# Mixture-of-experts layer of a graph network: the first aggregation's sums accumulated while the count matrix is still being filled, and the loads at the start reordered

## The chip, the cores and the metric

The kernel runs on one core of a Trainium2 chip. The metric is the device time of one execution in microseconds (us). TensorE (PE) multiplies matrices, VectorE (DVE) and ScalarE (ACT) work on elements, GpSimd (POOL) issues the indirect DMAs here, and SyncE (SP) and ACT issue the plain ones. PEld is the loading of weights into TensorE.

## The reference

Four graph layers follow one another on N = 6250 nodes with D = 128 features and 106250 edges, sorted by destination (50000 pairs in both directions and one loop per node). `src`, `dst` and `edge_type` are given.

```python
h = relu(layernorm(x))
x = x + L0(h)    # relu(segsum((h[src] + rel_emb[type]) @ Wn, dst) / sqrt(deg) + h @ W_loop)
h = relu(layernorm(x))
x = x + L1(h)    # mixture of experts, below
h = relu(layernorm(x))
x = x + L2(h)    # edge weights sigmoid(relu((h[dst]-h[src]) @ W1 + b1) @ w2 + b2)
h = relu(layernorm(x))
x = x + L3(h)    # three rounds of normalised mean aggregation

def L1(x):                       # 3 layers, H = 256, 4 weak and 4 strong experts
    h = x @ W_in + b_in
    for l in range(3):
        agg = segsum(h[src], dst) / deg
        logits = concat(h, agg) @ router_W[l] + router_b[l]
        # the two best experts of each node, softmax of their logits as gates
        moe = sum over the two of gate * expert(agg)
        h = h + sigmoid(h @ conf_W[l] + conf_b[l]) * moe
    return h @ W_out + b_out
```

## The kernel before, in words

**The count matrix.** All sums over edges are done as dense matrix products. The nodes are padded to 49 tiles of 128 (`NT`), and the destinations are cut into 13 blocks of 512 (`BW`, `NBLK`; the last has one tile). `adj` in device memory holds, for each block of destinations, a matrix of bytes: how many edges go from each source to each destination. An aggregation of a block loads groups of four source tiles (`AG1`, 256 KB, tile `ra_in`), turns bytes into numbers (`ra_r`, of type F32R), and multiplies each source tile's features with it. The features stand as two halves, a rounded one and the rest (`h2r`, `r2`), so that each tile costs two matmuls: 98 per block and 128 features.

**The first stage** (L302 to L576) makes the matrix and the first graph layer together. The matrix is cleared by SP (`clear`, L331, four DMAs of 784 KB per block from the tile `rzero`), two blocks ahead of the small loads, the rest after them. VectorE computes for each edge its place and its count (`places`, L429; 52 groups of 16 x 128 edges), with keys that ACT's queue loads (L409). POOL writes them with 832 indirect DMAs of 128 edges each (`scatter`, L462), from the last group to the first. A load of block b waits for the scatters that reach it. The loop over the blocks (L499) goes from the last to the first: the count of edge types per destination (`ct`, L512 to L525, some 79 matmuls behind one-hot tiles `oht` and `ohd` that VectorE makes), the degrees (L535 to L551), the aggregation (L553, `aggregate` at L262, whose casts are all on ACT at L276 there), the types' share (L283), a turning of h by TensorE (`transposed`, L286), the two products by weights (L567, L568), and x plus the result, whose normalised rows become `h` (L576). The output of the block's x goes to `x_d[0]`.

Before the loop, x is loaded as one tile `h` (L307, L308) by SP ahead of the first clears, normalised in place in seven steps of 7 tiles, and split into the halves `h2r` (L491 to L494).

**The mixture** (L582 to L948). For each of three layers, `first_step` (L601) goes over the blocks: `load` (L758) fetches `ra_in` on SP, VectorE and ACT share the casts (L801, L803), TensorE sums (L807; one part of 128 features in layer 0, which aggregates before the product by `W_in`, and two in the layers after). `inputs` (L608) makes h turned, `aggregated` (L636) scales the sums and in layer 0 multiplies them by `W_in` (L653), and `rest` (L658), a generator, does the routing: logits (`plt`, L665; turned into `plg`, L672), the two best experts (L684 to L711), the number of rows ahead of each (`pk`, L728, L729), and POOL's writes of the rows into the experts' lists (L743). The generator of block b - 1 is advanced among the groups of block b. In layer 0 the halves `r2` are made by `rows` (L767) from `h`; in the later layers the rows are loaded from `hf_d`, and `inputs` loads the block again as `rold` (L788) and transposes it (L632). `second_step` (L821) runs the experts over their lists.

**Order.** The program is written as a stream of tile operations; a scheduler at build time puts them into one fixed sequence per engine, by priority (in the order of the program, `tc.high_priority()` ahead) and by its own model of durations, and sets the waits. Each engine then runs its sequence in order. So an instruction that waits holds all that stands behind it on its engine or its queue. A pool (`tc.tile_pool`) gives memory back when it closes, and a tile that takes this memory waits for its last users.

The edge stage (L1033 on) uses `tloc` (L1059), made from `dloc`, the place of each edge's destination in its window, that the first stage kept.

## Time and profile before

| | |
|---|---|
| median of 3 runs | 6091.3 us (6075.11 to 6093.58) |
| profiled execution | 6081.65 us, span of its instructions 6079.9 us |
| PE busy | 4834.3 us (80%), 24167 instructions |
| DVE, ACT, POOL busy | 3079.4 us (51%), 2516.0 us (41%), 2525.5 us (42%) |
| mean granted TensorE clock | 0.901 |
| first scatter, last scatter (L465) starts | 54.9, 1155.4 us |
| router of layer 0: first aggregation matmul, last matmul of `first_step` (L924) | 1231.8, 1675.7 us |

The profile's groups give a line of the kernel, an engine, the operation with the tiles it writes and reads, the count, then the busy time and the mean of one in ns, and after the second bar the idle time of the engine just before these instructions with what ended it. Busy matmuls overlap, so the distance between starts says more than a mean duration. The slices of the page cut the span into 40 equal parts; each digit is a share in tenths. The clock is the share of TensorE's full rate that was granted.

### The profile page before, as it was taken

The numbers are of one execution on the slowest core, as the hardware profiler recorded it, in microseconds if no ns is written. First come the engines' busy times: TensorE is split into PE (matmuls) and PEld (weight loads), VectorE is DVE, ScalarE is ACT, GpSimd is POOL, SyncE is SP. The second block draws the span as 40 slices with busy tenths as digits, with TensorE's granted clock in tenths as the row PEclk, the third lists the DMA queues.
The fourth block names the chain that finished last, engine by engine and source line by source line (L and its number), as shares of the span: only waits on it lengthen the run. The fifth ranks groups of instructions, "written<-read, shape, count | busy, mean of one in ns | idle before, by whom it ended". The sixth has DMA issues, their size and how long they took to land. (4 is left out here: it accounts for less than half of the span.)

```text
span 6079.9 us, 76269 instructions
## 1 busy us (share of the span) xinstructions
PE 4834.3 (80%) x24167; PEld 3639.6 (60%) x24191; DVE 3079.4 (51%) x7850; ACT 2516.0 (41%) x5902; POOL 2525.5 (42%) x2376
## 2 busy tenths in 40 slices
PE   0186345599978899997879998986577878789999
PEld 0143223366656677775657776665556666678887
DVE  8975345554511333331133332116788888875555
ACT  2153233344322222222222222224678878855444
POOL 5777777422254211114521112361777777600000
PEclk9987677799989999998989998998678878899999
DMA  8234334455464533335653334467566666534454
GB/s 308 84 63 133 81 111 117 122 147 157 142 146 74 128 94 100 101 90 131 120 139 99 98 97 136 81 119 208 151 177 200 194 184 205 172 89 126 129 147 138
DMA packets 605630, 811.31 MB, mean 133 GB/s; under 512 B 116102, under 2 KB 402616, under 8 KB 605084
## 3 DMA queue, kind: packets, MB, share of 16 engines
q1 hardware_dynamic: 372740, 549.03, 30.5%
q0 software_dynamic: 132896, 194.37, 14.7%
q10 hardware_dynamic: 99448, 61.48, 3.8%
q8 instruction: 239, 3.92, 0.3%
q14 instruction: 307, 2.51, 0.2%
HBM read 594.70 MB, written 209.89 MB: 132 GB/s over the span
## 5 line engine op out<-in xcount | busy, mean ns | idle before, releaser
L807 PE MATMUL ragg<-ra_r,r 128*128 128x512 f32 (+1 forms) x6370 | 1471.5, 388 | 11.4 <-ACT r L777 10.5
L807 PEld LDWEIGHTS ragg<-ra_r,r 128*128 128x128 f32 x6370 | 1153.6, 190 | 270.9 <-issue 30.3
L1128 POOL DMA_INDIRECT rss<-rtab_s,rsrc_c x832 | 809.0, 972 | 376.5 <-DMA rx_d<-rv 111.5
L465 POOL DMA_INDIRECT adj<-rcnt,ixs x832 | 816.5, 981 | 285.6 <-issue 247.2
L743 POOL DMA_INDIRECT list_d<-rx,rpli x294 | 313.7, 1067 | 1439.0 <-issue 1184.5
L276 ACT CAST ra_r<-ra_in 128x1024 fp32r<-128x1024 uint8 (+3 forms) x494 | 543.9, 1113 | 776.5 <-DMA ra_in<-adj 422.2
L801 DVE CAST ra_r<-ra_in 128x1536 fp32r<-128x1536 uint8 (+4 forms) x507 | 388.0, 768 | 843.5 <-PE ragg L807 701.0
L803 ACT CAST ra_r<-ra_in 128x1024 fp32r<-128x1024 uint8 (+3 forms) x468 | 371.7, 797 | 1025.9 <-PE ragg L807 658.3
L882 POOL DMA_INDIRECT hf_d<-ry,rto x352 | 548.0, 1557 | 552.2 <-DVE ry L868 343.4
L279 PE MATMUL ragg<-ra_r,h 128*128 128x512 f32 (+1 forms) x1274 | 388.2, 447 | 324.9 <-ACT ra_r L276 324.9
L279 PEld LDWEIGHTS ragg<-ra_r,h 128*128 128x128 f32 x1274 | 241.6, 213 | 347.8 <-ACT ra_r L276 329.8
L1161 PE MATMUL acc<-mv,oh 128*128 128x258 f32 x1648 | 347.3, 354 | 112.4 <-DVE mv L1155 110.9
L274 DVE CAST ra_r<-ra_in 128x1024 fp32r<-128x1024 uint8 (+4 forms) x364 | 268.6, 744 | 249.9 <-PE ragg L279 237.1
L1161 PEld LDWEIGHTS acc<-mv,oh 128*128 128x128 f32 x1648 | 290.3, 238 | 152.9 <-DVE mv L1155 144.3
L1086 PE MATMUL rpart<-ra_r,cur 128*128 128x512 f32 (+1 forms) x1144 | 326.5, 413 | 51.7 <-ACT ra_r L1083 41.6
L1141 PE MATMUL pz<-gw,ohT 128*128 128x128 bf16 x2496 | 248.8, 259 | 125.8 <-DVE ohT L1133 69.4
L279 PE MATMUL ragg<-ra_r,cur 128*128 128x512 f32 (+1 forms) x1404 | 327.8, 393 | 6.2 <-DVE ra_r L274 6.2
L523 PE MATMUL ct<-ohd,oht 128*128 128x128 bf16 (+7 forms) x1024 | 204.9, 222 | 159.1 <-DVE ohd L521 149.5
L866 PE MATMUL rp<-st,rsh 128*128 128x256 f32 x1344 | 315.1, 383 | 18.3 <-DVE ry L868 18.3
L835 DVE COPY at<-rtr 128x512 f32<-128x512 f32 (+1 forms) x112 | 77.0, 687 | 489.8 <-PE rtr L834 489.8
L856 PE MATMUL rp<-at,st 128*128 128x512 f32 x672 | 302.1, 603 | 2.7 <-DVE roff L846 1.4
L1148 ACT ACTIVATE rz<-rz 128x128 f32<-128x128 f32 x832 | 245.9, 297 | 129.9 <-DVE rz L1144 129.3
(320 smaller groups left out, 7939.3 us busy)
## 6 DMA issues: line engine op xcount, KB each, us to landing
ra_in<-adj SPq DMA_DIRECT2D x1092, 256.0 KB
row<-list_d SPq DMA_DIRECT2D x111, 516.0 KB
list_d<-rzero SPq DMA_DIRECT2D x65, 774.0 KB
adj<-rzero SPq DMA_DIRECT2D x52, 784.0 KB
rd_b<-dst SPq DMA_DIRECT2D x208, 128.0 KB
gw<-rtab_d SPq DMA_DIRECT2D x208, 96.0 KB
adj<-rcnt,ixs POOLq DMA_INDIRECT x832
rss<-rtab_s,rsrc_c POOLq DMA_INDIRECT x832
```

Source lines behind the costliest of these rows:

```text
L276: nc.scalar.copy(ar[:, m:c, :w], a[:, m:c, :w])
L279: nc.tensor.matmul(ps[:, :w], rows2[:, s, g + k, :], ar[:, k, :w], start=(g + k == t0 and s == 0), stop=(not extra and g + k == NT - 1 and ...
L465: d = nc.gpsimd.indirect_dma_start(out=adj[0:(hi + 1) * ABS], out_offset=bass.IndirectOffsetOnAxis(ap=ixs[:, s, j:j + 1], axis=0), in_=cnt ...
L743: d = nc.gpsimd.indirect_dma_start(out=list_d[:], out_offset=bass.IndirectOffsetOnAxis(ap=pli[:, 2 * t + k:2 * t + k + 1], axis=0), in_=xs ...
L801: nc.vector.tensor_copy(ar[:, :m, :w], a[:, :m, :w])
L803: nc.scalar.copy(ar[:, m:c, :w], a[:, m:c, :w])
L807: nc.tensor.matmul(ps[:, h_, :w], r2[:, s, g + k, h_ * P:(h_ + 1) * P], ar[:, k, :w], start=(n == 0 and k == 0 and s == 0), stop=(n == len ...
L866: nc.tensor.matmul(p2_, sh[f][:, t * P:(t + 1) * P], st2[:, f, :], start=(f == 0), stop=False)
L882: d = nc.gpsimd.indirect_dma_start(out=hf_d[:], out_offset=bass.IndirectOffsetOnAxis(ap=to[:, t:t + 1], axis=0), in_=y[:, t, :], in_offset ...
L1086: nc.tensor.matmul(ps[:, :w], cur2[:, s, g + k, :], ar[:, k, :w], start=(g + k == t0 and s == 0), stop=(g + k == t1 - 1 and s == 1))
L1128: nc.gpsimd.indirect_dma_start(out=ss[:, k, 1:], out_offset=None, in_=tab_s[:], in_offset=bass.IndirectOffsetOnAxis(ap=src_c[:, g * WG + k ...
L1161: nc.tensor.matmul(acc[t], oh[:, k, n * P:(n + 1) * P], mv[:, k].rearrange("p s f -> p (s f)"), start=(g == ends[t][0] and k == 0), stop=( ...
```

## The change

* The normalised rows of the first stage's result are kept as two halves `h12` from the start (in place of `h` and, in the mixture's layer 0, `r2`), and a new tile `part1` holds sums of the mixture's first aggregation.
* In the loop of the first stage, `aggregate` is replaced by `sums0` and `more`. `sums0(b)` does the block's own 49 source tiles, and for the sources of blocks that are already done (above b, and not 0 or 1) it uses the same loaded and cast counts for a second sum with `h12`. `more(j, b + 2)` adds to each destination block j from b + 2 up the sources of block b + 2. After the loop, sources 2 to 12 of all destinations are summed. Casts take two tiles at a time (`counts`).
* The mixture's layer 0 sums only the sources of blocks 1 and 0 (`groups = [AG1, 0]`) and adds `part1` in `aggregated`.
* Turning h uses two matmuls with the identity on the two halves (`transposed2`) in place of a transpose, in the first stage and in layer 0; in layers 1 and 2 block 0 is turned from `r2` in this way, and its load `rold` falls away.
* The first clears: block 12, then three of the seven chunks of x (`x_rows`, 7 tiles each), then block 11. The other chunks of x are issued on ACT's queue as buffers come free.
* The identity and the tile of zeros get priority. `iota_f` is made later in a pool of its own, the biases of each mixture layer are built in a pool of their own, `dloc` is no longer kept (the edge stage loads `dst_cols` again), some buffers of the first stage go from two to one.

```diff
     ident = const.tile([P, P], F32, name="rident")
-    make_identity(nc, ident)
...
-    nc.vector.tensor_copy(ident_b, ident)
+    with tc.high_priority():
+        make_identity(nc, ident)
+        nc.vector.tensor_copy(ident_b, ident)
...
     nc.gpsimd.iota(iota8, pattern=[[1, 8]], base=0, channel_multiplier=0,
-                   allow_small_or_imprecise_dtypes=True)
-    iota_f = const.tile([P, P], F32, name="iota_f")
-    nc.gpsimd.iota(iota_f, pattern=[[1, P]], base=0, channel_multiplier=0,
...
     inv_r = const.tile([P, NT], F32, name="rinv_r")
-    dloc = const.tile([P, NCH], F32, name="dloc")
+    ident_r = const.tile([P, P], F32R, name="ident_r")
+    nc.vector.tensor_copy(ident_r, ident)
...
+    def transposed2(dst, rows2, b, psum):
+        nt = blk_tiles(b)
+        p = psum.tile([P, 4, P], F32, tag="mm", name="rtr")
+        for k in range(nt):
+            for s in range(2):
+                nc.tensor.matmul(p[:, k, :], rows2[:, s, 4 * b + k, :], ident_r, start=(s == 0), stop=(s == 1))
+        nc.scalar.copy(dst[:, :nt * P], p[:, :nt, :].rearrange("p t d -> p (t d)"))
...
-    h = hp.tile([P, NT, D], F32, name="rh0")
+    h12 = hp.tile([P, 2, NT, D], F32R, name="h12")
+    part1 = hp.tile([P, NBLK, BW], F32, name="part1")
...
-        nc.vector.memset(h[:, NT - 1, :], 0.0)
-        nc.sync.dma_start(h[:, :NT - 1, :], rows_of(i["x"], 0, NT - 1))
-        nc.sync.dma_start(h[:N - (NT - 1) * P, NT - 1, :], i["x"][(NT - 1) * P:N, :])
...
-        p2 = pool("rprep2", 2)
+        early = ExitStack()
+        p2 = early.enter_context(tc.tile_pool(name="rprep2", reuse_waits="tile", bufs=2))
+        h2r = pp.tile([P, 2, NT, D], F32R, name="h02")
+        XC = 7
+        def x_rows(g, eng):
+            xt = p2.tile([P, XC, D], F32, name="rxt", bufs=3)
+            full = min(XC, NT - 1 - g)
+            eng.dma_start(xt[:, :full, :], rows_of(i["x"], g, full))
+            if full < XC:
+                nc.vector.memset(xt[:, full], 0.0)
+                eng.dma_start(xt[:N - (NT - 1) * P, full, :], i["x"][(NT - 1) * P:N, :])
+            return xt
...
-        for b in (NBLK - 1, NBLK - 2):
-            clear(b)
+        clear(NBLK - 1)
+        xts = [x_rows(g, nc.sync) for g in range(0, 3 * XC, XC)]
+        clear(NBLK - 2)
...
-        h2r = pp.tile([P, 2, NT, D], F32R, name="h02")
...
-        for g in range(0, NT, 7):
-            norm_relu(h[:, g:g + 7], h[:, g:g + 7], 7, p2)
-            nc.scalar.copy(h2r[:, 0, g:g + 7], h[:, g:g + 7])
-            nc.vector.tensor_tensor(h2r[:, 1, g:g + 7], h[:, g:g + 7], h2r[:, 0, g:g + 7], ALU.subtract)
+        for n, g in enumerate(range(0, NT, XC)):
+            xt = xts[n]
+            norm_relu(xt, xt, XC, p2)
+            nc.scalar.copy(h2r[:, 0, g:g + XC], xt)
+            nc.vector.tensor_tensor(h2r[:, 1, g:g + XC], xt, h2r[:, 0, g:g + XC], ALU.subtract)
+            if 3 * XC + g < NT:
+                xts.append(x_rows(3 * XC + g, nc.scalar))
+        early.close()
+        lp = pool("rl0", 2)
...
+        def counts(b, c):
+            w = blk_tiles(b) * P
+            m = blk_tiles(c)
+            a = lp.tile([P, AG1, BW], U8, name="ra_in", tag="a_in", bufs=3)
+            nc.sync.dma_start(a[:, :m], adj_v[b][:, 4 * c:4 * c + m, :])
+            for k in range(0, m, 2):
+                n = min(2, m - k)
+                ar = lp.tile([P, 2, BW], F32R, name="ra_r", tag="a_r", bufs=4)
+                nc.scalar.copy(ar[:, :n, :w], a[:, k:k + n, :w])
+                yield 4 * c + k, [ar[:, q, :w] for q in range(n)]
+        def sums0(b, extra):
+            w = blk_tiles(b) * P
+            ps = ps_a.tile([P, BW], F32, name="ragg0")
+            done = list(range(NBLK - 1, max(b, 1), -1))
+            ps1 = ps_u.tile([P, BW], F32, name="rsum1") if done else None
+            blocks = [c for c in range(NBLK) if c not in done] + done
+            for c in blocks:
+                for t, ars in counts(b, c):
+                    for k, ar in enumerate(ars):
+                        for s in range(2):
+                            nc.tensor.matmul(ps[:, :w], h2r[:, s, t + k, :], ar,
+                                             start=(t + k == 0 and s == 0), stop=False)
+                    if c in done:
+                        for k, ar in enumerate(ars):
+                            for s in range(2):
+                                nc.tensor.matmul(ps1[:, :w], h12[:, s, t + k, :], ar,
+                                                 start=(c == done[0] and t + k == 4 * c and s == 0),
+                                                 stop=(c == done[-1] and t + k == 4 * c + blk_tiles(c) - 1 and s == 1))
+            for k, (lhs, rhs) in enumerate(extra):
+                for s in range(3):
+                    nc.tensor.matmul(ps[:, :w], lhs[:, s, :], rhs, start=False, stop=(k == len(extra) - 1 and s == 2))
+            if done:
+                nc.vector.tensor_copy(part1[:, b, :w], ps1[:, :w])
+            return ps
+        def more(b, c):
+            w = blk_tiles(b) * P
+            ps1 = ps_u.tile([P, BW], F32, name="rsum1")
+            for t, ars in counts(b, c):
+                for k, ar in enumerate(ars):
+                    for s in range(2):
+                        nc.tensor.matmul(ps1[:, :w], h12[:, s, t + k, :], ar, start=(t + k == 4 * c and s == 0),
+                                         stop=(t + k == 4 * c + blk_tiles(c) - 1 and s == 1))
+            if b == c == NBLK - 1:
+                nc.vector.tensor_copy(part1[:, b, :w], ps1[:, :w])
+            else:
+                nc.vector.tensor_tensor(part1[:, b, :w], part1[:, b, :w], ps1[:, :w], ALU.add)
...
-            ps, _ = aggregate(b, lp, ps_a, h2r, 0, 3, [(rel3[:, k], ty[:, k, :w]) for k in range(TYT)], True)
+            if b + 2 < NBLK:
+                for j in range(b + 2, NBLK):
+                    more(j, b + 2)
+            ps = sums0(b, [(rel3[:, k], ty[:, k, :w]) for k in range(TYT)])
...
             nc.vector.tensor_copy(ag[:, :w], ps[:, :w])
-            hT = lp.tile([P, BW], F32, name="rhT0")
-            transposed(hT, h, b, ps_m)
+            hT = lp.tile([P, BW], F32, name="rhT0", bufs=1)
+            transposed2(hT, h2r, b, ps_m)
...
             nc.scalar.dma_start(rows_of(x_d[0], 4 * b, nt), xb[:, :nt])
-            norm_relu(h[:, ts], xb, nt, lp)
+            norm_relu(r, xb, nt, lp)
+            split_halves(h12[:, 0, ts], h12[:, 1, ts], r[:, :nt])
...
     tri = wp.tile([P, P], BF16, name="tri")
-    nc.vector.tensor_scalar(tri, iota_f, iota_p, None, op0=ALU.is_gt)
+    with tc.tile_pool(name="rtri", reuse_waits="tile", bufs=1) as tp:
+        iota_f = tp.tile([P, P], F32, name="iota_f")
+        nc.gpsimd.iota(iota_f, pattern=[[1, P]], base=0, channel_multiplier=0,
+                       allow_small_or_imprecise_dtypes=True)
+        nc.vector.tensor_scalar(tri, iota_f, iota_p, None, op0=ALU.is_gt)
...
                 xT = ap.tile([P, BW], F32, name="rxT")
-                transposed(xT, h, b, ps_m)
+                transposed2(xT, h12, b, ps_m)
...
             else:
-                old = olds[b]
...
+                    fs = slice(f * P, (f + 1) * P)
...
-                        nc.tensor.transpose(p[:, t, :], old[:, t, f * P:(f + 1) * P], ident)
+                        if b:
+                            nc.tensor.transpose(p[:, t, :], olds[b][:, t, fs], ident)
+                            continue
+                        for s in range(2):
+                            nc.tensor.matmul(p[:, t, :], r2[:, s, t, fs], ident_r, start=(s == 0), stop=(s == 1))
...
             u = ap.tile([P, BW], F32, name="ru")
-            nc.vector.tensor_tensor(u[:, :w], ps[:, 0, :w], iv[:, :w], ALU.mult)
+            nc.vector.tensor_tensor(u[:, :w], ps[:, 0, :w], part1[:, b, :w], ALU.add)
+            nc.vector.tensor_tensor(u[:, :w], u[:, :w], iv[:, :w], ALU.mult)
...
-        groups = list(range(0, NT, AG1))
-        if not l:
-            groups.reverse()
+        groups = list(range(0, NT, AG1)) if l else [AG1, 0]
...
             ts = slice(4 * k, 4 * k + nt)
-            if not l:
-                nc.scalar.copy(r2[:, 0, ts], h[:, ts])
-                nc.vector.tensor_tensor(r2[:, 1, ts], h[:, ts], r2[:, 0, ts], ALU.subtract)
-                return
...
             w = nt * P
-            if l:
+            if l and b:
...
                 c = min(AG1, NT - g)
-                if b == 0:
+                if l and b == 0:
...
         bias = wp.tile([P, BW], BF16, name="rbias", bufs=2)
-        bias_rows(bias, [
+        with tc.tile_pool(name=f"rbs{l}", reuse_waits="tile", bufs=1) as bs:
+          bias_rows(bias, [
...
-            (4, 1, slice(8, 9), i["L1_gnn_conf_b"][l:l + 1, :])], BW, wp, "bs")
+            (4, 1, slice(8, 9), i["L1_gnn_conf_b"][l:l + 1, :])], BW, bs, "bs")
...
-            r2 = rp.tile([P, 2, NT, H if l else D], F32R, name=f"r2{l}")
+            r2 = rp.tile([P, 2, NT, H], F32R, name=f"r2{l}") if l else h12
...
         nc.vector.tensor_scalar(base, base, float(NP - P), None, op0=ALU.min)
-        nc.vector.tensor_scalar(base, base, P - 1, None, op0=ALU.bitwise_and)
-        nc.vector.tensor_tensor(tloc, dloc.rearrange("p (g k) -> p g k", k=WG), base, ALU.add)
+        nc.vector.tensor_scalar(base, base, 7, 7, op0=ALU.logical_shift_right, op1=ALU.logical_shift_left)
+        dst_c = ep.tile([P, NWG, WG], I32, name="rdst_c2", bufs=1)
+        nc.sync.dma_start(dst_c.rearrange("p g k -> p (g k)"), i["dst_cols"])
+        nc.vector.tensor_tensor(tloc, dst_c, base, ALU.subtract)
...
```

More of the change, by code (lines that the diff above doesn't have):

```diff
@@ L217, in norm_relu @@
         nc.vector.tensor_scalar(nm[:, :nt], s[:, :nt], -1.0 / D, None, op0=ALU.mult)
-        sq = pool.tile([P, D], F32, name="rln_sq")
         v = small.tile([P, 7], F32, name="rln_v")
         for t in range(nt):
+            sq = pool.tile([P, D], F32, name="rln_sq") if dst is src else dst[:, t, :]
             nc.scalar.activation(sq, src[:, t, :], AF.Square, bias=nm[:, t:t + 1], accum_out=v[:, t:t + 1])
@@ L328, in regular_path @@
         zero = pp.tile([P, zn // 4], F32, name="rzero")
-        nc.vector.memset(zero, 0.0)
+        with tc.high_priority():
+            nc.vector.memset(zero, 0.0)
         def clear(b):
@@ L347, in regular_path @@
             nc.sync.dma_start(dst_c.rearrange("p g k -> p (g k)"), i["dst_cols"])
-            typ_c = cp.tile([P, NCH], I32, name="rtyp_c")
+            typ_c = cp.tile([P, NCH], I32, name="rtyp_c", tag="c")
             nc.sync.dma_start(typ_c, i["typ_cols"])
-            base = cp.tile([P, NWG, WG], I32, name="rbase")
+            base = typ_f.bitcast(I32).rearrange("p (g k) -> p g k", k=WG)
             nc.gpsimd.iota(base, pattern=[[241, NWG], [0, WG]], base=0, channel_multiplier=0)
@@ L354, in regular_path @@
             nc.vector.tensor_scalar(base, base, float(NP - P), None, op0=ALU.min)
-            nc.vector.tensor_tensor(dloc.rearrange("p (g k) -> p g k", k=WG), dst_c, base, ALU.subtract)
-            typ_t = cp.tile([P, NCH], I32, name="rtyp_t")
-            nc.vector.tensor_scalar(typ_t, typ_c, P - 1, None, op0=ALU.bitwise_and)
-            as_number(typ_f.bitcast(I32), typ_t)
-            nc.vector.tensor_scalar(typ_c, typ_c, 7, None, op0=ALU.logical_shift_right)
-            nc.vector.tensor_scalar(typ_c, typ_c, 6.0, 127.0, op0=ALU.mult, op1=ALU.add)
-            nc.vector.tensor_scalar(typ_v.bitcast(I32), typ_c, 23, None, op0=ALU.logical_shift_left)
-            dloc_i = cp.tile([P, NCH], I32, name="dloc_i")
-            nc.vector.tensor_copy(dloc_i, dloc)
-            as_number(dloc_f.bitcast(I32), dloc_i)
-            dst_r = cp.tile([P, NCH], I32, name="rdst_r")
+            nc.vector.tensor_tensor(dst_c, dst_c, base, ALU.subtract)
+            as_number(dloc_f.bitcast(I32), dst_c.rearrange("p g k -> p (g k)"))
+            tv = typ_v.bitcast(I32)
+            nc.vector.tensor_scalar(tv, typ_c, 7, None, op0=ALU.logical_shift_right)
+            nc.vector.tensor_scalar(tv, tv, 6.0, 127.0, op0=ALU.mult, op1=ALU.add)
+            nc.vector.tensor_scalar(tv, tv, 23, None, op0=ALU.logical_shift_left)
+            nc.vector.tensor_scalar(typ_c, typ_c, P - 1, None, op0=ALU.bitwise_and)
+            as_number(typ_f.bitcast(I32), typ_c)
+            dst_r = cp.tile([P, NCH], I32, name="rdst_r", tag="c")
             nc.sync.dma_start(dst_r, i["dst_flat"].rearrange("(p c) -> p c", c=NCH))
@@ L385, in regular_path @@
         QG = 4
-        lp = pool("rl0", 2)
         ps_c = pool("ps_c", 2, space=bass.MemoryType.PSUM)
         ps_a = pool("ps_a0", 1, space=bass.MemoryType.PSUM)
+        ps_u = pool("ps_u0", 2, space=bass.MemoryType.PSUM)
         ps_m = pool("ps_m0", 2, space=bass.MemoryType.PSUM)
@@ L525, in regular_path @@
                                      skip_group_check=True)
-            ci = lp.tile([P, BW], I32, name="rci")
+            ci = lp.tile([P, BW], I32, name="rci", bufs=1)
             nc.vector.tensor_copy(ci[:, :w], ct[:, :w])
-            ty = lp.tile([P, TYT, BW], BF16, name="rty")
+            ty = lp.tile([P, TYT, BW], BF16, name="rty", bufs=1)
             for q in range(TYT):
-                tyi = lp.tile([P, BW], I32, name="rtyi")
+                tyi = lp.tile([P, BW], I32, name="rtyi", bufs=1)
                 nc.vector.tensor_scalar(tyi[:, :w], ci[:, :w], 6 * q, 63, op0=ALU.logical_shift_right,
```

## The prediction

> **What bounds the kernel now.** I first read the slices of the page, then the stretches of 100 us that hold the two stages of the change, then the groups, then single instructions around the hand-over. From the page's slices (152 us each):
>
> ```profile
> PE   0186345599978899997879998986577878789999
> ...
> POOL 5777777422254211114521112361777777600000
> PEclk9987677799989999998989998998678878899999
> ```
>
> Slices 2 to 7 are the first stage: POOL is as busy as it ever is, TensorE half idle and at a lower clock. From slice 8 TensorE is full. The stretches say it more sharply (start and end; busy us and instructions of PE, PEld, DVE, ACT, POOL; clock, DMA share, GB/s):
>
> ```profile
> 700.00:800.00 100.00, 39.54 (x187) 24.27 (x187) 37.77 (x113) 26.59 (x28) 75.00 (x78) 0.67 0.34 93
> 1000.00:1100.00 100.00, 43.41 (x240) 27.11 (x240) 39.67 (x121) 26.64 (x31) 74.33 (x77) 0.72 0.37 89
> ...
> 1400.00:1500.00 100.00, 99.84 (x423) 67.98 (x425) 51.79 (x153) 42.24 (x67) 24.89 (x22) 1.00 0.51 149
> ```
>
> In the first stage no other engine is full and POOL issues 77 scatters per 100 us; its busy 75 us are durations, the gaps of 0.30 us between its instructions make up the rest. In the router stage TensorE leaves nothing free at clock 1.00. The groups name the waits:
>
> ```profile
> L465 POOL DMA_INDIRECT adj<-rcnt,ixs x832 | 816.5, 981 | 285.6 <-issue 247.2
> ...
> L276 ACT CAST ra_r<-ra_in 128x1024 fp32r<-128x1024 uint8 (+3 forms) x494 | 543.9, 1113 | 776.5 <-DMA ra_in<-adj 422.2
> ...
> L279 PE MATMUL ragg<-ra_r,h 128*128 128x512 f32 (+1 forms) x1274 | 388.2, 447 | 324.9 <-ACT ra_r L276 324.9
> ```
>
> Scatter: (816.5 + 285.6)/832 = 1.32 us each, 1102 us in all. ACT waits 422 us for loads of the count matrix (they wait for the scatter of their block) and TensorE waits 325 us for ACT. So stage one is set by POOL, and TensorE has room in it. The end of the stage:
>
> ```profile
> 1155.42 0.96 POOL L465 DMA_INDIRECT adj<-rcnt,ixs  x1 [0.30 <-issue]
> 1205.04 0.59 POOL L192 DMA_DIRECT2D bias_f<-in_L_gnn_weak_b  x1 [48.66 <-DVE rtyi L531]
> ```
>
> ```profile
> 1160.26 1.90 ACT L276 CAST ra_r<-ra_in 128x2048 fp32r<-128x2048 uint8 x1 [28.48 <-DMA ra_in<-adj]
> ```
>
> The last scatter is issued at 1155.4, block 0's first cast starts at 1160.3, and the router's first aggregation matmul at 1231.8. Earlier long waits of this kind end at 544.7, 633.0, 737.9, 820.9, 906.6, 991.2, 1096.0 and 1160.3: (1160.3 - 544.7)/7 = 87.9 us per block, 64 to 105 singly. And the router, one block's end to end:
>
> ```profile
> 1423.72 10.26 PE L807 MATMUL ragg<-ra_r,r 128*128 128x512 f32 x44
> 1433.86 2.20 PE L653 MATMUL rpa<-ru,rw_in 128*128 128x512 f32 x4
> ...
> 1458.43 10.26 PE L807 MATMUL ragg<-ra_r,r 128*128 128x512 f32 x44
> 1468.58 2.20 PE L653 MATMUL rpa<-ru,rw_in 128*128 128x512 f32 x4
> ```
>
> ```profile
> 1659.79 7.88 PE L807 MATMUL ragg<-ra_r,r 128*128 128x128 f32 x36
> ```
>
> A block takes 1468.58 - 1433.86 = 34.7 us. A 512-column matmul goes every (1433.86 - 1423.72)/44 = 0.23 us; a 128-column one of the same kind takes 7.88/36 = 0.22 us, hardly less.
>
> **What is removed and moved.** The first aggregation of the mixture is 13 blocks x 49 tiles x 2 halves = 1274 matmuls. Sources 2 to 12 (13 x (40 + 1) x 2 = 1066) move into stage one; 208 stay, 16 per block.
>
> (1) *Router.* Of 34.7 us, 98 x 0.23 = 22.5 are aggregation, 12.2 the other matmuls. Left: 16 x 0.23 = 3.7, plus 12.2, plus the new turning. Four transposes of `transposed` (0.09 us apart) become eight 128-column matmuls at 0.22: 1.8 - 0.4 = +1.4. Floor 17.3 us. DVE and ACT are below that: DVE 51.8% and ACT 42.2% of 34.7 are 18.0 and 14.7 us, less some 9 and 8 us of casts, plus the addition of `part1` (0.69, row L650) on DVE. POOL has 8 list scatters, 11.7 us. Upper end: nothing covers the hand-overs that those matmuls cover now: plg to pk 7.3 us less 0.7 of other PE work, xT 1.2, u 1.2 and the new addition 0.7, the copies of rag 1.5, lt 1.1; together 12.3, so 29.6 us. I take 21: the profile shows these holes filled by the next block's matmuls (4 to 16 at a time), and the next block's `inputs` and its 16 sums remain to fill some. Twelve blocks: 12 x 13.7 = 164. The 128-column block 12 loses 82 x 0.22 = 18, of which I count 10, since its closing chain then shows. **Gain 174** (ends: 12 x 17.4 + 18 = 227; 12 x 5.1 = 61). Hidden with it: 143 loads and their casts, and the 13 pairs of operations at L772/L773.
>
> (2) *Stage one, POOL-bound.* Count k = 12 - b. Block b has 98 + 8k matmuls that share casts, and 8(k-1) for `more`. Other TensorE work per block: ct 79 x 0.12 = 9.5 (four in 0.40 to 0.54 us when none waits), L283 12 x 0.43 = 5.2, the rest 3.5: 18 us. At k = 8: 218 x 0.23 + 18 = 68 us; k = 11: 266 x 0.23 + 18 = 79; k = 12: 274 x 0.23 + 18 = 81. All are below the pace of 87.9, so for most blocks the cover is the wait for the scatter. What remains is the end. From block 2 on (991.2 to 1160.3, 169 us) TensorE has sums of 178 and 186, `more` of 80 and 88 matmuls: 532 x 0.23 = 122, two times 18, and some 10 us per block of hand-overs now seen between blocks: 178 us. So it comes about 9 late to block 0; I take **12** (0 if `more` fits in the idle times, 40 if it is ordered behind the loads that wait). Block 0 itself does 88 more: **+20**. Its last turning and the new split into halves (0.69 as a copy of 128x512 at L561, 0.65 as the subtraction at L773): **+3**. ACT per late block: 25 + 22 casts of 128x1024 at 0.95 = 45 us, and 13 others: below 64, so it doesn't set the pace.
>
> (3) *POOL's pace.* 66 more loads of 256 KB, 17 MB. Between 500 and 600 us, with DMA share 0.52, POOL issued 73 instead of 77 to 78 per 100 us. The loads raise the share by about 0.05 over 700 us: one percent or two of 1102: **+10** (0 to 25).
>
> (4) *The start.* The first scatter starts at 54.9; before it POOL waited 24.9 us for the column load that SP issues behind x (3.2 MB) and two blocks of clears (6.4 MB). Afterwards 1.4 MB of x and the clears are ahead: 1.8 MB at some 300 GB/s: **-6** (0 to -10). The rest of x goes through ACT's queue, which also loads the keys; a wait there for a free `rxt` holds the key loads behind it. DVE makes places four times as fast as POOL uses them (all by about 290 us): 0. The loop's pool `lp` now opens where that of the places closes, so that block 12's sums, whose casts ran from 170.8 us, may have to wait until 290; that is some 25 us for the first blocks, and the waits of 26.2 and 32.1 us that end at 458.7 and 544.7 take them up: 0, and up to 25 without that cover. The early identity: 0, hidden by the same wait.
>
> (5) *Later layers.* Block 0's turning is 16 matmuls of 0.22 = 3.5 us within busy PE, where 8 transposes ran in the wait for `rold` (PE idle 11.6 and 25.2 us until then). Against it one load fewer ahead of `rres`: **+2** for both (-4 to +10). Biases from a scoped pool: 12 short POOL loads at 0.52 per layer, now at worst after the previous step: in these ends. The edge stage computes `tloc` at 4117.6 and first uses it at 4225.4: the additional load is hidden; counted **+1** for its queue.
>
> Sum: -174 + 12 + 20 + 3 + 10 - 6 + 2 + 1 = **-132**. The profiled execution took 6081.65 us (span 6079.9), 9.7 below the median of the runs shown (6091.3; 6075.1 to 6093.6). 6081.65 - 132 = **5950**, by the median 5959; I say 5950.
>
> **A rule against it.** Granted clock: 0.67 to 0.72 with TensorE 40% busy (rows above), 1.00 where it is full. The Trainium skill, "TensorE: Matmul & The Clock Gate", section "HAM oscillation", says that idle gaps over about 3.4 us put the array back to half clock. For a router with gaps that would be an estimated 34.6 us of PE per block by that page, and no gain there; the same rule quickens stage one, whose gaps shrink. No row here shows the thinned router.
>
> **Rivals.**
> *Full filling* (0.17): the order covers all hand-overs, 17.3 us per block, and TensorE is on time for block 0: 5950 - 53 - 12 = 5885. For it: TensorE was busy 99.8% in the router. Against: only 16 sums per block are left to fill with.
> *The chain takes the place of the sums* (0.15): 29.6 us per block, gain 61: 5950 + 113 = 6063. For it: the chain of 7.3 us on DVE and single buffers (riz, ru, lt). Against: two blocks are in flight.
> *Stage one becomes TensorE-bound* (0.08): the matmuls there stay at the clock of 0.70 of the rows, 0.23/0.70 = 0.33 each, 18/0.70 = 26 others and 10 hand-overs: from k = 5 on a block exceeds 87.9, and the excess (29.7 + 5.3k - 52) adds up to 182 us for k = 5 to 12. In place of the 12 + 20: 5950 + 182 - 32 = 6100, slower. It decides from some 0.32 us per matmul on. Against: clock 1.00 returns within each run of matmuls, which stand 0.23 apart in the rows of 1115 to 1136 us too.
> *Forecast* (0.60): 5890 to 6030.
>
> That the change doesn't do what it says is the extreme of the third: were the moved sums ordered behind the waits throughout, the 1066 would come back as 1066 x 0.23 = 245 us in place of those 32, 6163.
>
> **How the numbers follow.** Range 5870 to 6068: it takes in both faster rivals and leaves out the third and the tails, some 0.2. Within 0.3% (18 us, about what a measurement of this kernel tells from no change) falls a part of the second rival: 0.04. Faster 0.87, slower 0.09.
>
> **What would show it.** In the new profile: first scatter near 49; 832 of them in 1100 to 1125 us; PE busy over 70% between 700 and 1100; router's first list matmuls near 1270; blocks of 21 us there, its end near 1545. Wrong if scatters slow below 73 per 100 us, if PE's clock in late stage one stays near 0.7, or if a router block takes over 27 us.

## The result, and the profile after

The changed kernel takes 6053.82 us (median of 5 runs, 6046.39 to 6057.58) against 6091.3 (5 runs, 6075.11 to 6094.58): a ratio of 0.9943, interval [0.9929, 0.9957]. It is faster, by 37 us; the forecast was 132 to 141. The profiled execution took 6053.65 us (span 6051.9). Seven of the runs below (e6, e7, e8, e1r, e6r, e7r, e8r) fell in a condition in which DVE started some one operation per scatter of POOL in stage one (72 of each per 100 us in e1r) and the kernel before itself took 7067 to 7080 us, so they are compared only with one another.

Slices of the changed kernel's page, and three rows of its table by stretches of 100 us (busy us and instructions of PE, PEld, DVE, ACT and POOL, then the granted clock, the DMA share and GB/s):

```profile
PE   0088787878698899989879998976577878799999
...
POOL 6777777303454211114611113462777777600000
PEclk9998787888799999999989999998778879899999
```

```profile
700.00:800.00 100.00, 80.14 (x357) 55.56 (x356) 45.25 (x133) 41.05 (x56) 75.50 (x78) 0.80 0.45 131
...
1000.00:1100.00 100.00, 79.15 (x364) 55.40 (x362) 46.63 (x135) 47.93 (x63) 75.11 (x78) 0.81 0.38 100
...
1200.00:1300.00 100.00, 80.52 (x361) 56.98 (x360) 41.97 (x117) 47.49 (x62) 0.00 (x0) 0.81 0.35 104
```

From 600 to 1300 us TensorE is 79 to 82% busy in each 100 us; before, it was 40 to 47% busy from 600 to 1100. That was forecast. The last row was not: POOL has nothing left between 1200 and 1300 us, and TensorE goes on at the same 361 instructions per 100 us. Stage one no longer ends with POOL. The waits between 300 and 1330 us say it too (who waited, for what, us in total, times, longest):

```profile
ACT ra_r L530 <- PE rsum L567: 213.2, 18, 27.4
POOL iota_f L669 <- PE ragg L545: 192.8, 1, 192.8
...
PE ct L598 <- DVE ohd L596: 97.5, 152, 2.2
```

After its last scatter POOL waits 192.8 us for the last sums of stage one. In the page's groups of instructions, the casts' wait for counts has become smaller (422.2 before, 240.3 now, of which 128.1 is the one ahead of the first cast at 301), and so has the sums' idle time (324.9, of which 138.4 ahead of the first sum; now 53.8):

```profile
L484 POOL DMA_INDIRECT adj<-rcnt,ixs x832 | 812.9, 977 | 283.6 <-issue 238.7
...
L530 ACT CAST ra_r<-ra_in 128x1024 fp32r<-128x1024 uint8 (+3 forms) x456 | 426.5, 967 | 592.1 <-DMA ra_in<-adj 240.3
L545 PE MATMUL ragg<-ra_r,h 128*128 128x512 f32 (+1 forms) x1274 | 372.3, 430 | 53.8 <-ACT ra_r L530 53.7
...
L598 PE MATMUL ct<-ohd,oht 128*128 128x128 bf16 (+7 forms) x1024 | 212.0, 233 | 371.8 <-DVE ohd L596 363.7
```

The counts of relations (`ct`, L598; L523 before) now wait 363.7 us for DVE's one-hots, against 149.5. Most of both is a single wait ahead of the first of them (265.6 us now, 94.8 before). Without it 98 us stand against 55, and the 97.5 us from 300 us on are the longest sum of waits that TensorE has left. What this costs is seen from the starts of a few instructions in four profiles (us from the span's start; e1 and e2 are explained below):

| | before | e2: no moved sums | after | e1: sums ahead of ct |
|---|---|---|---|---|
| first scatter | 54.9 | 45.4 | 45.3 | 45.1 |
| last scatter | 1155.4 | 1138.7 | 1126.1 | 1139.4 |
| router's first sum | 1231.8 | 1215.9 | 1342.9 | 1243.5 |
| router's last matmul | 1675.7 | 1663.4 | 1622.0 | 1522.0 |
| first turning of a list | 1690.6 | 1678.2 | 1640.9 | 1541.1 |
| second layer's first sum | 2098.0 | 2088.8 | 2054.7 | 1950.6 |
| third layer's first sum | 3094.8 | 3094.7 | 3064.4 | 2960.0 |
| end of the span | 6079.9 | 6077.6 | 6051.9 | 5954.8 |

From before to after: the router starts 111.1 us later and is 443.9 - 279.1 = 164.8 shorter; between its last matmul and the last turning of a list in the third layer 25.2 are lost (4.0 at the first lists, 8.4 ahead of the third layer's sums, the rest in pieces of up to 6), and 0.5 behind it: 111.1 - 164.8 + 25.2 + 0.5 = -28.0, the difference of the spans.

**One late block.** The timeline of TensorE in the changed kernel, from the block that closes at 1104.67 to the next one's first sum (start, us, instruction, in brackets the idle time before it and what ended it):

```profile
1104.67 2.76 PE L555 MATMUL ragg<-rty,rel 128*128 128x512 bf16 x12
...
1115.15 0.97 PE L598 MATMUL ct<-ohd,oht 128*128 128x128 bf16 x4 [0.56 <-DVE ohd L596]
1116.75 0.97 PE L598 MATMUL ct<-ohd,oht 128*128 128x128 bf16 x4 [0.63 <-DVE ohd L596]
...
1142.12 0.93 PE L598 MATMUL ct<-ohd,oht 128*128 128x19 bf16 x4 [0.65 <-DVE ohd L596]
1143.57 4.32 PE L567 MATMUL rsum<-ra_r,h 128*128 128x512 f32 x12 [0.52 <-DVE part L572]
...
1168.10 2.50 PE L545 MATMUL ragg<-ra_r,h 128*128 128x512 f32 x5 [7.30 <-ACT ra_r L530]
```

And DVE in that stretch:

```profile
1114.16 0.68 DVE L592 TENSOR_TENSOR oht<-seen,typ_f 128x512 bf16<-128x512 bf16 x1
1114.76 1.09 DVE L596 TENSOR_SCALAR ohd<-seen,dloc_f,typ_v 128x128 bf16<-128x128 bf16 x4
1115.77 0.68 DVE L592 TENSOR_TENSOR oht<-seen,typ_f 128x512 bf16<-128x512 bf16 x1
...
1142.72 0.70 DVE L572 TENSOR_TENSOR part<-part,rsum 128x512 f32<-128x512 f32 x1
```

DVE makes the one-hots of a window every 1115.77 - 1114.16 = 1.61 us, and TensorE takes four matmuls per window at that pace, with nothing in between, from 1114 to 1143: 29 us. It counts as busy for 0.97 of each 1.61, or 60%, so that a block of which DVE paces a part comes to read as 80% busy. The moved sums that could lie between stand still: `more` (L567) has two PSUM buffers, both are full, and the additions that empty them (L572) stand in DVE's queue behind the block's one-hots, since `ct` comes first in the program. The first addition starts at 1142.72, and at 1143.57 `more` goes on. From close to close the last six blocks take 94.1, 96.3, 103.5, 105.2, 108.1 and 108.3 us: more than POOL's 87.9.

### The profile page after: what moved, and what is told of

Same layout as the page of the kernel before. It is cut to its first block, busy times and chain, and to the rows that moved or that the text cites. A ratio compares the mean times of both kernels' runs of the same rounds, so it can differ in the third digit from the quotient of the medians.

```text
span 6051.9 us, 76470 instructions
## 1 busy us (share of the span) xinstructions
PE 4926.0 (81%) x24305; PEld 3705.4 (61%) x24305; DVE 3027.5 (50%) x7811; ACT 2549.7 (42%) x6046; POOL 2506.7 (41%) x2376
## 5 line engine op out<-in xcount | busy, mean ns | idle before, releaser
L889 PE MATMUL ragg<-ra_r,r 128*128 128x512 f32 (+1 forms) x5096 | 1161.4, 386 | 57.3 <-ACT r L859 57.0
L889 PEld LDWEIGHTS ragg<-ra_r,r 128*128 128x128 f32 x5096 | 921.0, 189 | 259.3 <-ACT r L859 58.1
L831 POOL DMA_INDIRECT list_d<-rx,rpli x294 | 299.9, 1020 | 1317.5 <-issue 953.8
L530 ACT CAST ra_r<-ra_in 128x1024 fp32r<-128x1024 uint8 (+3 forms) x456 | 426.5, 967 | 592.1 <-DMA ra_in<-adj 240.3
L883 DVE CAST ra_r<-ra_in 128x1024 fp32r<-128x1024 uint8 (+4 forms) x364 | 278.3, 765 | 780.4 <-PE ragg L889 636.4
L885 ACT CAST ra_r<-ra_in 128x1024 fp32r<-128x1024 uint8 (+1 forms) x338 | 269.3, 797 | 870.4 <-PE ragg L889 542.6
L598 PE MATMUL ct<-ohd,oht 128*128 128x128 bf16 (+7 forms) x1024 | 212.0, 233 | 371.8 <-DVE ohd L596 363.7
L545 PE MATMUL ragg<-ra_r,h 128*128 128x512 f32 (+1 forms) x1274 | 372.3, 430 | 53.8 <-ACT ra_r L530 53.7
L598 PEld LDWEIGHTS <-oht 128*128 128x128 bf16 x1024 | 95.5, 102 | 504.6 <-DVE oht L592 382.8
L272 DVE CAST ra_r<-ra_in 128x1024 fp32r<-128x1024 uint8 (+4 forms) x364 | 268.6, 744 | 251.7 <-PE ragg L277 239.3
L274 ACT CAST ra_r<-ra_in 128x512 fp32r<-128x512 uint8 (+3 forms) x325 | 259.8, 806 | 300.4 <-PE ragg L277 240.3
```

Source lines behind the costliest of these rows:

```text
L530: nc.scalar.copy(ar[:, :n, :w], a[:, k:k + n, :w])
L545: nc.tensor.matmul(ps[:, :w], h2r[:, s, t + k, :], ar, start=(t + k == 0 and s == 0), stop=False)
L598: nc.tensor.matmul(ct[:, lo:hi], oht[:, k, :], ohd[:, k, off:off + hi - lo], start=(n == 0 and k == 0), stop=(n == len(wins) - 1 and k == ...
L889: nc.tensor.matmul(ps[:, h_, :w], r2[:, s, g + k, h_ * P:(h_ + 1) * P], ar[:, k, :w], start=(n == 0 and k == 0 and s == 0), stop=(n == len ...
```

## The experiments

**Theory T:** a late block is set by `ct` at DVE's pace, with nothing beside it. **R1:** TensorE has too many matmuls at its clock of 0.81. **R2:** the waits for the counts' loads (7 to 8 us per block). **R3:** the sums start at 300 instead of 170 us, and that is never made good.

### e1: the moved sums ahead of the counts

```diff
+            if b + 2 < NBLK:
+                for j in range(b + 2, NBLK):
+                    more(j, b + 2)
+
             ct = ps_c.tile([P, BW], F32, name="ct")
             wins = windows_of(b)
...
-            if b + 2 < NBLK:
-                for j in range(b + 2, NBLK):
-                    more(j, b + 2)
             ps = sums0(b, [(rel3[:, k], ty[:, k, :w]) for k in range(TYT)])
```

> The changed kernel with one thing moved: the additional sums (more) stand ahead of the counts of relations (ct) in the program, so that DVE's additions to part1 come ahead of the one-hots and TensorE can do moved sums while it waits for one-hots. Same instructions, another order. Theory T (ct, paced by DVE at some 1.61 us per window and now beside nothing, is what makes a late block 103 to 108 us): TensorE's stretch of ct alone (29 us) goes, late blocks come down to 80 to 90 us, the router's first sums start at 1230 to 1280 instead of 1343, and the time falls by 60 to 110 us below the changed kernel's, to 5945 to 5995. Rival R1 (TensorE has too many matmuls at its clock of 0.81): the number of matmuls and their clock are the same, so within 15 us of the changed kernel. Rival R2 (the wait for the counts' loads, 7 to 8 us per block): stays, within 15 us. Rival R3 (the first sums start at 300 instead of 170 us and that is never made good): a part of it returns at most, 0 to 40 us.

Measured: 5956.95 us (5 runs) against 6093.98 for the kernel before, ratio 0.9776 [0.9763, 0.979]. Late blocks take 99.5, 84.5, 85.0, 87.8, 110.0 and 84.1 us. TensorE in e1 now puts single matmuls of `ct` between the sums, and in the block that takes 110.0 it waits for counts of freshly scattered blocks again, as before the change:

```profile
1053.40 0.22 PE L602 MATMUL ct<-ohd,oht 128*128 128x109 bf16 x1
1053.43 1.18 PE L567 MATMUL rsum<-ra_r,h 128*128 128x512 f32 x4
...
1084.91 2.50 PE L545 MATMUL ragg<-ra_r,h 128*128 128x512 f32 x5 [21.20 <-ACT ra_r L530]
```

```profile
1000.00:1100.00 100.00, 71.69 (x349) 48.53 (x349) 44.83 (x123) 44.94 (x60) 71.03 (x74) 0.85 0.38 113
1100.00:1200.00 100.00, 95.50 (x482) 64.96 (x482) 59.45 (x165) 57.29 (x72) 31.43 (x35) 0.97 0.46 128
```

Between 1100 and 1200 us, where the scatters end, TensorE does 482 instructions in 100 us at a clock of 0.97, where the changed kernel did 364 at 0.81. Its waits for one-hots from 300 us on fall from 97.5 us to 11.5. The same matmuls in another order are 97 us faster: R1 and R2 fall.

R3 is settled for e1 alone. Its first sums start at 302 as well, but block 5's own sums wait 30.6 us for their counts, until 724.1, so the late start has been made good by then. In the changed kernel no block's own sums wait for POOL after the start: block 5's own sums begin at 754.8, 43 us after the last scatter that its counts need (711.7), and in the other blocks that distance is longer. By these starts an earlier begin could have moved the whole stage by up to some 40 us (an estimate); no run tried it.

### e1b: priority for the additions alone

```diff
-                nc.vector.tensor_tensor(part1[:, b, :w], part1[:, b, :w], ps1[:, :w], ALU.add)
+                with tc.high_priority():
+                    nc.vector.tensor_tensor(part1[:, b, :w], part1[:, b, :w], ps1[:, :w], ALU.add)
```

> The changed kernel with the additions to part1 alone given priority on DVE; the program's order is as it was. Theory T, in the form that DVE's queue (one-hots ahead of the additions) and the two PSUM buffers hold the moved sums up: the same as with the order changed, 60 to 110 us below the changed kernel. If not the queue but the order of TensorE itself holds them up, 0 to 30 us. Rivals R1 and R2: within 15 us.

Measured: 5967.59 us, ratio 0.9786 [0.9773, 0.98]; the router's first sum at 1250.8. So the place of the additions in DVE's queue is enough: with the program's order unchanged, 86 us come back. The intervals of e1 and e1b overlap.

### e2: the change without the moved sums

```diff
-            done = list(range(NBLK - 1, max(b, 1), -1))
+            done = []
...
-        groups = list(range(0, NT, AG1)) if l else [AG1, 0]
+        groups = list(range(0, NT, AG1))
```

(`more` and the addition of `part1` in the router are left out with it.)

> The changed kernel without the moved sums: the router does all 1274 matmuls again; the early identity, the order of the first loads, the late opening of the pool lp, the turning from the halves, and block 0's turning in the later layers stay. Theory T: stage one bound by POOL again with the cover of the sums over ct as before, first scatter some 10 us earlier than before, router as long as before plus 13 turnings (10 to 20 us), later layers as in the changed kernel: 5 below to 25 us above the kernel before, 6085 to 6115. Rival R3 (late start of the first sums is carried to the end): the router starts 50 us or more later than before, 6140 or more.

Measured: 6083.59 us, ratio 0.9983 [0.9974, 0.9993], 10 us below the kernel before and just below the 6085 to 6115 that were expected. The loads in another order, the late pool and the turnings together are worth that little; the rest is the moved sums'. Against e2, they cost stage one 1342.9 - 1215.9 = 127.0 us in the changed kernel and 27.6 in e1, and take 447.5 - 279.1 = 168.4 from the router.

### e3: the kernel before with late first sums

```diff
+        early.close()
+        lp = pool("rl0", 2)
```

(behind the normalisation of x; `early` holds the pool of the places, and `lp` opened ahead of them.)

> The kernel before with one edit: the pool of the places closes before the pool lp opens, as in the changed kernel, so that block 12's sums start late. Theory T: the waits for the scatters take it up, within 10 us of the kernel before. Rival R3: the router starts later by 50 us or more, and the time rises by as much.

Measured: 6092.3 us, ratio 0.9991 [0.9982, 1.0001], and the router's first sum comes at 1232.8 instead of 1231.8. Two rows of its page:

```profile
L279 PE MATMUL ragg<-ra_r,h 128*128 128x512 f32 (+1 forms) x1274 | 393.7, 450 | 184.4 <-ACT ra_r L276 184.2
L525 PE MATMUL ct<-ohd,oht 128*128 128x128 bf16 (+7 forms) x1024 | 205.1, 223 | 321.1 <-DVE ohd L523 311.4
```

The sums' idle time is 184.4 us instead of 324.9 only because the wait ahead of the first of them (138.4 us before) now stands at `ct`, whose first matmul waits 260.8. Where the late start went is seen from the casts' waits for counts: the first long one is 11.7 us and ends at 463.9, where it was 26.2 and ended at 458.7, and the next ends at 550.1 instead of 544.7. From there the casts follow the scatters as before. In the kernel before, the late start comes out of these waits, as the prediction had it; for the changed kernel, which has no such waits, e3 shows nothing.

### e8, e8r, e8s: fewer one-hots

```diff
-                oht = lp.tile([P, WG, P], BF16, name="oht")
...
+                if n == 0:
+                    oht = lp.tile([P, WG, P], BF16, name="oht")
...
```

(The operation that fills `oht` moves under the same condition.)

> The changed kernel with one of DVE's two kinds of one-hots (oht, 0.69 us per window) built once per block instead of once per window; this leaves out a part of the computation (the counts of relations are taken for the first window's types alone). TensorE's instructions are all there, in the program's old order. Theory T (a late block is set by DVE's pace in the stretch of ct): a window takes about 1.1 us instead of 1.61, a late block some 8 to 10 us less, and the time falls by 40 to 80 us below the changed kernel's 6054. Rival R1 (number and clock of TensorE's matmuls) and rival R2 (loads): within 10 us of it.

> e8 once more (oht built once per block; the counts of relations are left wrong by that). Theory T: a window of ct at about 1.1 us instead of 1.61, late blocks 8 to 10 us shorter, 40 to 80 us below the changed kernel. R1 and R2: within 10 us of it.

> e8 again, on a chip where the kernel before takes about 6090 us if this is one (oht built once per block; the counts of relations are left wrong by that). Theory T: a window of ct in some 1.1 us instead of 1.61, late blocks 8 to 10 us shorter, 40 to 80 us below the changed kernel on the same chip. R1 and R2: within 10 us of it.

> The changed kernel itself beside the others on the same chip: 0.993 to 0.996 of the kernel before where that takes about 6090 us. Where it takes about 7070 us (there DVE's operations in the first stage come one per scatter of POOL) theory T gives the same order among the kernels: e8 and the changed kernel some 100 us above e1.

e8 and e8r, in the condition told above, took 7237.02 us (before 7080.39) and 7230.35 (before 7066.94), and the changed kernel didn't run beside them: nothing follows. Outside that condition e8s took 5959.41 us, ratio 0.9803 [0.9788, 0.9818], the changed kernel beside it (afts) 6041.52, ratio 0.9934 [0.9917, 0.995]: 82 us less, a little over what T gave. The last five blocks take 85.4, 90.8, 92.9, 96.7 and 98.1 us against 96.6, 100.7, 105.5, 107.0 and 105.9: 8 to 13 us each. All of TensorE's instructions are there in the program's old order; it is DVE's work that sets these blocks.

### e6, e7 and their repeats: the loss ahead of the third layer

In after, e1, e1b and e2 the third layer's first sum comes 50 to 52 us behind the last turning of the second layer's lists, before 43.9. The first theory, Q, blamed the later layers' block 0, whose turning no longer needs a load.

```diff
-                        if b:
-                            nc.tensor.transpose(p[:, t, :], olds[b][:, t, fs], ident)
-                            continue
-                        for s in range(2):
-                            nc.tensor.matmul(p[:, t, :], r2[:, s, t, fs], ident_r, start=(s == 0), stop=(s == 1))
+                        nc.tensor.transpose(p[:, t, :], olds[b][:, t, fs], ident)
```

(e6; in e7 the load of `olds[b + 1]` stands at the last group of block b instead. Both with e1's order.)

> The kernel with the sums ahead of the counts (e1), and block 0 of the two later layers turned from the rows read (rold), as in the kernel before. It asks for the 7 us that the third layer's first sums come later after the last turning of the lists than before (50 to 52 us against 43.9). Theory Q: with block 0's rold load gone, both buffers are free and the rold loads of blocks 1 and 2 are issued 7 us after the first rres loads and share the DMA engines with them; undone, the gap is 44 us again and the time 4 to 9 us below e1's. Rival Q2: the biases' loads from the scoped pool are the cause; the gap stays at 50 to 52, within 3 us of e1.

> The kernel with the sums ahead of the counts (e1), block 0 turned from the halves as in the changed kernel, and the rold load of each following block placed in program order at the last group of the block before it. Theory Q: the first rres loads have the DMA engines for themselves, the gap before the third layer's first sums falls from 51 to 36 to 45 us, and the time lies 5 to 15 us below e1's, if no later block waits for its rold. Rival Q2: within 3 us of e1, the gap unchanged.

> The kernel with the sums ahead of the counts (e1) once more, as the base on the same chip for the three below: 0.976 to 0.979 of the kernel before.

> e6 once more on the same chip as its base e1. Theory Q: the gap before the third layer's first sums 44 us instead of 50 to 52, and 4 to 9 us below e1. Rival Q2: gap unchanged, within 3 us.

> e7 once more on the same chip as its base e1. Theory Q: the gap falls to 36 to 45 us, 5 to 15 us below e1. Rival Q2: gap unchanged, within 3 us.

Measured: e6 7139.65 us, e7 7144.89; e1r 7127.95, e6r 7125.58, e7r 7130.79. For e1r 0.976 to 0.979 of the kernel before were expected, and it took 1.0092 [1.0077, 1.0107] of it: in that condition e1's order is slower than the kernel before. There TensorE does nothing between 100 and 900 us (e1r); what causes the condition is open. The gaps are 56.0 (e6), 56.2 (e6r), 50.3 (e7), 51.1 (e7r) and 52.1 (e1r). Neither closes it, and e6, which undoes the edit, has a longer one. Q falls as far as these runs, all in that condition, can tell.

### e9: biases in tiles that stay

What ends the wait is in e1's profile. ACT's first cast into `r2` and DVE's split of the layer's biases:

```profile
2958.90 2.94 ACT L860 CAST r<-rres 128x1024 fp32r<-128x1024 f32 x3 [8.88 <-DMA rold<-hf_d]
```

```profile
2956.10 0.43 DVE L191 CAST rbias<-bias_f 128x512 bf16<-128x512 f32 x1 [6.43 <-DMA bias_f<-in_L_gnn_conf_b]
...
2958.07 0.68 DVE L196 TENSOR_TENSOR rbias<-bias_f,bias_mid 32x512 bf16<-32x512 f32 x1
```

The profile names a DMA for the cast, but the cast starts 0.15 us after the split's last operation (2958.07 + 0.68 = 2958.75). So the theory is that `r2` lies where the scoped pool of the biases lay, whose loads POOL issues only behind the second step's last scatter (from 2942.39 on).

```diff
-        with tc.tile_pool(name=f"rbs{l}", reuse_waits="tile", bufs=1) as bs:
+        with ExitStack() as scoped:
+          bs = kept if l else scoped.enter_context(tc.tile_pool(name="rbs0", reuse_waits="tile", bufs=1))
...
             l1h.close()
+            kept = l1.enter_context(tc.tile_pool(name="rbs1", reuse_waits="tile", bufs=1))
```

> The kernel with the sums ahead of the counts (e1), and the biases of the second and third layer built in tiles that stay, instead of in a pool that each layer opens and closes (there the tiles lie where the second step's had lain, and r2 of the layer is laid over them). Theory Q2: the biases can be loaded and split while the layer before still runs, r2's first write no longer waits for the last addition of the split, and the gap between the last turning of the lists and the third layer's first sums falls from 51 to 52 us to 44, the time by 5 to 9 us below e1 on the same chip. If the gap has another cause, 50 to 52 us and within 3 us of e1.

> The kernel with the sums ahead of the counts (e1), as the base on the same chip: 0.976 to 0.979 of the kernel before where that takes about 6090 us, 1.009 where it takes about 7070.

Measured: the gap is 45.0 us in e9 and 50.5 in e1s, beside it; TensorE's first sum behind it in e9:

```profile
2939.22 0.79 PE L890 MATMUL ragg<-ra_r,r 128*128 128x512 f32 x1 [31.84 <-ACT r L860]
```

In e1s that bracket holds 37.69. e9 takes 5931.21 us, ratio 0.9759 [0.9746, 0.9772]; e1s 5941.96, 0.9779 [0.9766, 0.9792]. That these 5.5 us of the gap come from the scoped pool is shown; of the 10.8 between the medians the intervals, which overlap, don't decide the rest. e9 beats both kernels of the study.

## Why the prediction was wrong

The sign held, and so did the range, by luck: it reached up to 6068 for the sake of a slow router, which did not come. The gain was little more than a quarter of the forecast's (37 of 132 to 141 us).

**(1) The router: right.** -174 forecast, -164.8 measured. A block takes 21.8 us on average, forecast 21, and the twelve blocks' 0.8 are the difference. The hole that the upper end named is there, shorter than feared. TensorE's groups between 1343 and 1622 us:

```profile
L889 PE MATMUL ragg<-ra_r,h 128*128 128x512 f32 (+1 forms) x208 | 53.9, 396 | 1.6 <-DVE ra_r L883 1.6
...
L816 PE MATMUL rpk<-rmask,tri 128*128 128x64 bf16 (+1 forms) x13 | 2.6, 203 | 52.0 <-DVE rmask L791 51.9
```

The wait for DVE's `rmask` is 51.9 us in twelve blocks, 4.3 each, where 6.6 were the upper end. The turnings cost less than put: e2, with all 1274 matmuls, has a router 3.6 us longer than before, where 13 x 1.4 = 18 were forecast; the eight matmuls of a turning start 0.11 us apart, and 0.22 were put.

**(2) Stage one: the step that failed.** +35 forecast, +127.0 measured against e2. The failed step is "Other TensorE work per block: ct 79 x 0.12 = 9.5 (four in 0.40 to 0.54 us when none waits)", and with it "All are below the pace of 87.9, so for most blocks the cover is the wait for the scatter". 9.5 us is what `ct` takes of TensorE's time between other matmuls. Before, it ran while the sums' counts were waited for (the casts' 422.2 us), and DVE's pace cost nothing. The prediction asked what the moved sums would hide behind, and not what hides `ct` once nothing waits for scatters. Nor did it follow DVE's queue, in which the additions that free `more`'s buffers stand behind the one-hots, so that the moved sums could not fill the stretch themselves; e1b shows that this place in the queue decides. By the pace of 1.61 us, 79/4 = 20 windows are 32 us instead of 9.5: at k = 11, 79 + 22.5 = 102 us, and the changed kernel's last blocks take 103.5 to 108.3. How much of the 127.0 is the late start of the first sums, which nothing makes good in the changed kernel, is open. With `ct` covered (e1) the term is 27.6.

e1's 5957 stands beside the 5950 to 5959 that were forecast for the changed kernel, but in part by luck: against the kernel before, its router starts 11.7 us later, where +35 + 10 - 6 = +39 were forecast; the router itself gives 165.4 of the 174, and all that follows it takes 28.6 us more, where +3 were.

Two readings of the prediction were too large without deciding anything. Of the 325 us for which TensorE waits for ACT, 138.4 lie ahead of its first sum. And 98 + 8k counts six matmuls too many per block, since block 12 has one tile: 6 x 0.23 = 1.4 us.

**(3) POOL's pace:** +10 forecast, 1 measured. POOL's first scatter to its last takes 1094.3 us with the additional loads (e1) and 1093.3 without (e2); in the changed kernel 1080.8, below the 1100.5 of before. There the end of POOL was no longer the end of the stage, so this gave nothing.

**(4) The start:** -6 forecast, the first scatter comes 9.6 earlier; e2, which has this edit and not the moved sums, is 10 us faster. The late pool costs nothing in the kernel before (e3); in the changed kernel that is not shown.

**(5) Later layers:** +2 forecast (ends -4 to +10). Found are 4.0 us at the first layer's lists, where POOL's list scatters end 9 us behind the shortened router instead of 3, and 8.4 ahead of the third layer's sums. Most of the latter (5.5 us in e9) is the biases' pool, which the prediction put "in these ends" without a price; undoing block 0's turning, which it priced, didn't close the gap (e6). Other pieces, 6 us in the first layer's experts above all (381.3 before, 387.2 after), vary nearly as much between e3, e1 and e2 (380.3, 383.2, 384.8) and are left open.

**The rivals.** "Stage one becomes TensorE-bound" has the right place and the wrong mechanism: its 0.33 us per matmul would last through any order, and e1 does the same matmuls at clocks of 0.82 to 0.97 per 100 us. Nearer was the extreme told with it, the moved sums "ordered behind the waits throughout", at 245 us: they did stand behind waits, of DVE's queue, for 127 in place of 245. It got no chance of its own.

**What would show it.** The router's blocks came as forecast, the first scatter 4 us earlier than the mark (45.3 for 49), the scatters faster than theirs (1080.8 for 1100 to 1125). "PE busy over 70% between 700 and 1100" held and misled: the 80% included `ct` at DVE's pace. The three signs of being wrong did not come either: 77 to 79 scatters per 100 us from 600 to 1100, a clock of 0.80 to 0.85 there, and 21.8 us per router block. The mark that decided was the router's first sum, 1342.9 instead of 1270.

What no run tried is a third PSUM buffer for `more`, or the changed kernel with its first sums at the old time.

## What to carry to other kernels

When work is moved beside other work, list for each stretch that stays what covered it before, and price it uncovered at the pace of its slowest engine, not at the time that it takes of the engine in question. Then follow the order inside each queue: a short operation that frees a buffer, behind a long row of others in program order, stops everything that needs the buffer, and moving it costs one line. A busy share of 80% doesn't show an engine at its limit; instructions per 100 us beside it do.

## What the runs showed of the hardware

Additional loads of 17 MB from the region that POOL scatters into, 58 of the 66 issued before the last scatter in e1, did not slow the scatters: 832 of them take 1094.3 us in e1, 1085.2 in e1s and 1100.2 in e1b, against 1093.3 without these loads (e2).

The thinned router kept most of its clock. Its row in the changed kernel:

```profile
1350.00:1600.00 250.00, 206.18 (x791) 111.36 (x792) 112.53 (x469) 75.83 (x148) 80.45 (x81) 0.89 0.36 110
```

This clock of 0.89 is a mixture. A stretch around one wait for `rmask` (5.33 us, until 1419.13) and the stretch behind it:

```profile
1416.10:1422.80 6.70, 3.67 (x7) 1.49 (x7) 4.93 (x30) 0.21 (x1) 0.00 (x0) 0.50 0.13 39
1422.90:1439.90 17.00, 14.41 (x63) 8.08 (x62) 6.05 (x19) 6.67 (x12) 7.91 (x8) 1.00 0.42 139
```

The clock is 0.50 ten times between 1350 and 1600 us, for 3.4 or 6.8 us each, 55 us in all, and 1.00 between. The Trainium skill, "TensorE: Matmul & The Clock Gate", section "HAM oscillation", has idle gaps over about 3.4 us bring the half clock back. The trace agrees: each of the seven gaps of 3.5 to 5.4 us in this stretch goes with half clock, and so do two of the three of 2.4 to 3.4 us. What does not come out is the prediction's estimate of 34.6 us per block, which took the half clock for the whole block; a block takes 21.8 us, since the clock is back after 7 us at most.

In stage one the clock followed the filling: 0.81 in the changed kernel, where DVE paces TensorE, and 0.97 in e1's filled stretch.
